# A graph transformer layer: the weighted sums take two slots per matmul, edge chunks go from five slots to six, and the prologue's matmuls are issued ahead of their evictions

## The chip, the cores and the metric

The kernel runs on one core of a Trainium2 chip. The metric is the time on the device, in microseconds (us), of one execution of the whole program; before the change it is the median of three runs.

The engines are called PE (TensorE, matrix products), Vector or DVE, ACT (ScalarE), POOL (GpSimd) and SP (SyncE, which here only issues DMAs). Transfers that are issued by POOL and gather or scatter rows by an index are called indirect DMAs. PSUM is the accumulator memory that PE writes[...].

## What is computed

One layer of a graph transformer over 6250 nodes with 256 features in float32. The 206,250 edges are sorted by destination and contain a self loop for each node, so a node has about 33 incoming edges.

```python
xn = layernorm(x)
# graph attention over the edges, 8 heads of 32
q, k, v = (xn @ W.T + b for W, b in ((Wq, bq), (Wk, bk), (Wv, bv)))
sim  = einsum('hed,hed->eh', q[:, dst], k[:, src]) * scale
p    = exp(sim - segment_max(sim, dst)[dst])
attn = p / segment_sum(p, dst)[dst]
agg  = segment_sum(attn * v[src], dst) @ Wo.T + bo
# linear attention over all nodes, 8 heads of 64, keys and values with instance norm
mix  = (qm @ (km.T @ vm) / 6250) @ w_out.T + b_out
x    = x + agg + mix
# top-1 mixture of 8 experts, 256 -> 1024 -> 256, each with a capacity of 1.25 * 6250 / 8
x    = x + experts(layernorm(x))
```

## The kernel before, in words

**Layout of the edges.** A block is 128 nodes, one in each partition; there are 49 blocks (`NB`). The nodes are ranked by their number of edges, so that the nodes of one block have about equally many. The ranking is done in three groups of 20, 17 and 12 blocks (`GROUPS`, L31). A block has as many slots as its longest node has edges; slot j of a block holds the j-th edge of each of its 128 nodes. The blocks have 1715 slots together, most of them 24 to 43, and three 62. A slot is one indirect DMA on POOL (L602): 128 rows of 512 float32, key and value, taken from the table `kv_tab` in device memory by the source indices `idx`. A block of more than 44 slots (`PART`) is cut into two units; there are 52 units. A unit is cut evenly into chunks of at most `W` = 5 slots (L559), 366 chunks in all, and a chunk is a tile `kvg` of the pool `kvp`, which has `RING` = 11 buffers (L25, L26, L202).

**Prologue.** For each block b, PE forms keys and values, `bank<-wn,xT` (L519, two matmuls of 512 columns, each of which appears in the trace as two records), Vector evicts them with norm and bias, `kv<-bank,rstd,bn` (L530), and SP writes them to `kv_tab` (L533). The statistics of the layer norm are made on ACT from rows of x, `xg`; these and the transposed x, `xT`, come by `load_x` (L368), four blocks at a time, issued by ACT's queue. Between the blocks `index_step` (L501) takes a piece of the ranking of the first group: `rank_group` (L266), with Vector's `lo`, `hi` and `rhs` (L332, L337, L344) and the matmuls that take them (L348). All of PE's products here take banks of the pool `bps` (five banks, function `bank`, L208), in the order in which the program gives them. Then POOL gathers the chunks of the first unit, while PE, Vector and SP do the same for the queries (L616, L620, L623) into `q_tab`. Both kinds of rows lie in three buffers (`ap3`) on their way out. Last, POOL gathers the queries of the first two blocks, and the loop begins.

**The loop over units.** It runs as if the unit before and the present one were interleaved. In one iteration, with c as the number of the chunk in each unit:

1. `weigh(v, c)` for the unit before: Vector multiplies the chunk's values by the weights `pr` (L1283), and PE adds the slots up by an identity matrix, 256 columns a slot, into `pa` in PSUM (L1287). The chunk's buffer is free after that.
2. `gather_to(at + 1 + LEAD)`: POOL issues the gathers of the chunk that lies `LEAD` = 2 chunks ahead, which needs a free buffer of the ring.
3. Scores of the present unit: Vector multiplies the keys by the queries (L1329) and reduces by head (L1330) into `sim`.

Around these steps `background` takes pieces of other work from a list: the ranking of the other groups, the linear attention, and, when a group of blocks has been sent, its output projection, routing, experts and last sum (`behind`, L1230). How much it takes at a time follows from `pace`, a hand-made estimate. After a unit's chunks come its maximum, the exponentials `pr` (L1347) and then `complete(v)` for the unit before: Vector multiplies `pa` by the inverse sums `s` into `ag` (L1303), and POOL scatters `ag` to the table `agg_tab` (`send`, `spaced_scatter`, L801). Each engine takes its instructions in the order in which the program issues them, POOL with its gathers and scatters too. So a scatter that waits for `ag` holds up the gathers behind it, and a unit with n chunks keeps n buffers of the ring until its weighing, one iteration after another, gives them back.

**The end.** The experts of the last group come after all gathers; their weights are loaded through the buffers of the same ring, `AHEAD` = 7 phases before their use (L1093). The kernel also has a general path for inputs that do not fit the plan; it does not run here.

Of the kernel before, what the change touches and what calls it, by code (L numbers as in the profile page):

```python
# [18 lines left out]
P = 128  # L19
# [5 lines left out]
W = 5  # L25
RING = 11  # L26
# [42 lines left out]
def gps_layer(  # L69
# [82 lines left out]
    with tc.manual_schedule():  # L152
# [52 lines left out]
        qps = mctx.enter_context(tc.tile_pool(name="qps", bufs=1, space=PSUM))  # L205
# [153 lines left out]
        with ExitStack() as actx:  # L359
            ap1 = actx.enter_context(tc.tile_pool(name="a1", bufs=1))  # L360
            ap2 = actx.enter_context(tc.tile_pool(name="a2", bufs=2))
            ap3 = actx.enter_context(tc.tile_pool(name="a3", bufs=3))

# [4 lines left out]
            def load_x(k, rows_too=True, queue=nc.scalar):  # L368
# [5 lines left out]
                if rows_too:  # L374
                    xg = ap2.tile([P, GX, D], F32, name="xg")
                    xgs[k] = xg
                    full = n
                    if b0 + n == NB:
                        full = n - 1
                        nc.vector.memset(xg[:, full, :], 0.0)  # L380
                        queue.dma_start(xg[:tail, full, :], x[(NB - 1) * P : N, :])
                    if full:
                        queue.dma_start(
                            xg[:, :full, :], x[b0 * P : (b0 + full) * P, :].rearrange("(t p) d -> p t d", p=P)
                        )
# [10 lines left out]
            load_x(0, queue=nc.sync)  # L396
            bn = ap1.tile([P, 3 * D], F32, name="bn")
            nc.sync.dma_start(bn, bcast_row(b_node, 3 * D))
            load_x(1, queue=nc.sync)
            for c in range(DC):  # L400
                nc.sync.dma_start(wn[:, c, 2 * D :], w_node[c * P : (c + 1) * P, 2 * D : 3 * D])
            load_x(2, queue=nc.sync)
# [110 lines left out]

            stat_end(0)
            for b in range(NB):
                k = b // GX
                pkv = bank((2 * D,))
                for c in range(DC):
                    nc.tensor.matmul(  # L519
                        pkv, xTs[k][:, b % GX, c, :], wn[:, c, : 2 * D], start=(c == 0), stop=(c == DC - 1)  # L520
                    )
                if b % GX == 0 and k + 1 < NGX:
                    stat_square(k + 1)
                if b % GX == GX - 1 and k + 1 < NGX:
                    stat_end(k + 1)
                    load_x(k + 3)
                    if k + 2 < NGX:
                        stat_sum(k + 2)
                kv = ap3.tile([P, 2 * D], F32, name="kv")
                nc.vector.scalar_tensor_tensor(  # L530
                    kv, pkv, rstd[:, b : b + 1], bn[:, : 2 * D], op0=ALU.mult, op1=ALU.add
                )
                nc.sync.dma_start(kv_tab[b * P : (b + 1) * P, :], kv)  # L533
# [18 lines left out]
            for b in order:  # L552
# [3 lines left out]
                for i in range(n_p):  # L556
                    n = cut[i + 1] - cut[i]
                    n_ch = -(-n // W)
                    cuts = [cut[i] + n * k // n_ch for k in range(n_ch + 1)]  # L559
# [52 lines left out]
            for b in range(NB):  # L612
                k = b // GX
                pq = bank((D,))
                for c in range(DC):
                    nc.tensor.matmul(  # L616
                        pq, xTs[k][:, b % GX, c, :], wn[:, c, 2 * D :], start=(c == 0), stop=(c == DC - 1)
                    )
                q = ap3.tile([P, 2 * D], F32, name="kv")[:, :D]
                nc.vector.scalar_tensor_tensor(  # L620
                    q, pq, rstd[:, b : b + 1], bn[:, 2 * D :], op0=ALU.mult, op1=ALU.add
                )
                nc.sync.dma_start(q_tab[b * P : (b + 1) * P, :], q)  # L623
                if b % GX == GX - 1:
                    load_x(k + 3, False)
# [8 lines left out]

        bctx = ExitStack()
# [444 lines left out]
        def experts(gi):  # L1080
# [12 lines left out]
            AHEAD = 7 if last else 2  # L1093
# [180 lines left out]
        def weigh(v, c):  # L1274
# [4 lines left out]
            if c == 0:  # L1279
                v["pa"] = qps.tile([P, D], F32, name="pa")  # L1280
# [5 lines left out]
            for j in range(m):  # L1286
                nc.tensor.matmul(v["pa"], ident, kv[:, j, D:], start=(j0 + j == s0), stop=(j0 + j == s1 - 1))  # L1287

        def complete(v):

            if v["part"] + 1 < v["parts"]:
                nc.vector.tensor_copy(v["acc"], v["pa"])
                return
            ag = cp3.tile([P, D], F32, name="ag")
            pa = v["pa"]
            if v["part"]:
# [4 lines left out]
                nc.vector.tensor_add(old, old, pa)  # L1301
                pa = old
            nc.vector.tensor_tensor(  # L1303
                heads(ag), heads(pa), v["s"][:, :, None].to_broadcast([P, GH, GD]), ALU.mult
# [613 lines left out]
```

## Time and profile before

The profiler took one execution; it is a good deal longer than the runs without it.

| what | value |
|---|---|
| time, median of three runs | 3119.5 us (3118.4 to 3120.74) |
| the profiled execution | 3534.2 us |
| its span, first to last instruction | 3532.3 us |
| mean granted TensorE clock in it | 0.812 |
| DMA | 730.28 MB, mean 207 GB/s |
| of it the gathers and scatters by POOL (software queue) | 477.83 MB, 44.4% of 16 engines |
| keys and values in the prologue | 13 to 156 us |
| queries in the prologue | 157 to 248 us |
| first scores | at 253 us |
| last gather | at 3206 us |
| experts of the last group | from 3341 us |

By stage, with the busy time of each engine, its number of instructions, the granted clock of PE, the share of the 16 DMA engines and the GB/s moved:

| stage, us | PE | Vector | ACT | POOL | clock | DMA | GB/s |
|---|---|---|---|---|---|---|---|
| 0 to 157 | 118.82 | 75.89 | 60.59 | 49.60 (58) | 0.85 | 0.59 | 188 |
| 157 to 250 | 53.93 | 26.75 | 0.00 | 36.43 (39) | 0.79 | 0.74 | 241 |
| 250 to 1000 | 461.18 | 550.03 | 155.02 | 456.90 (491) | 0.79 | 0.60 | 183 |
| 1000 to 2000 | 649.61 | 633.12 | 158.53 | 626.39 (692) | 0.81 | 0.67 | 207 |
| 2000 to 3000 | 694.10 | 573.52 | 140.02 | 600.46 (661) | 0.82 | 0.69 | 224 |
| 3000 to 3240 | 171.64 | 125.14 | 33.07 | 125.79 (138) | 0.81 | 0.61 | 199 |
| 3240 to 3532 | 188.45 | 39.07 | 86.62 | 24.39 (36) | 0.84 | 0.60 | 214 |

How to read the page: a group of instructions is named by its line, its engine and the tiles that it writes and reads, `pa<-kvg,ident`; then come the number of instructions, their busy time, the mean of one in ns, and the idle time of the engine just before them with what ended most of it. "issue" is idle time that ended with nothing the profile shows. The busy time of POOL's indirect DMAs is the time to issue them, not that of the transfer.

### The profile page before, as it was taken

Reading aid. Unit: us, or ns where it says so; the run is one execution under the profiler, and the core shown is the slowest. Engines: PE = TensorE matmul, PEld = TensorE weight load, DVE = VectorE, ACT = ScalarE, POOL = GpSimd, SP = SyncE. Lnnn points to the kernel's source line nnn. Section 1 sums busy time; section 2 is a strip of 40 time slices with the busy share of each in tenths; the row PEclk is TensorE's granted clock in tenths of the full one; section 3 lists DMA queues with packets and bytes.
Section 4 is the critical chain, followed back from the end, with each engine's and each line's share of the span. In section 5 each row is a group of like instructions: output and inputs, shape, how many; then the busy total and the mean of one; then the engine's idle time right before and its main releaser. Section 6 shows DMA issues by size and latency. Waiting matters only on the chain.

```text
span 3532.3 us, 29535 instructions
## 1 busy us (share of the span) xinstructions
PE 2337.7 (66%) x9086; PEld 1777.0 (50%) x9086; DVE 2023.5 (57%) x2723; ACT 633.9 (18%) x1802; POOL 1920.0 (54%) x2114
## 2 busy tenths in 40 slices
PE   7844457775767643764688887743664988866395
PEld 3433335443444432553576676622543877755394
DVE  4438677776767756676565654555673655545200
ACT  4200013322323200220111111110210111111142
POOL 4243656665666656656665665566546665552101
PEclk8876678888888876896798898866876999887697
DMA  6563956655655655775777776565756887664584
GB/s 215 197 205 103 332 156 182 181 173 168 181 172 176 185 160 167 240 218 176 254 253 241 241 247 230 183 195 176 234 162 215 287 271 255 237 201 139 199 321 141
DMA packets 291643, 730.28 MB, mean 207 GB/s; under 512 B 46838, under 2 KB 152020, under 8 KB 278164
## 3 DMA queue, kind: packets, MB, share of 16 engines
q0 software_dynamic: 149744, 477.83, 44.4%
q1 hardware_dynamic: 133560, 234.37, 18.9%
q10 hardware_dynamic: 8172, 16.10, 1.5%
q8 instruction: 75, 1.23, 0.1%
q14 instruction: 92, 0.75, 0.1%
HBM read 654.47 MB, written 73.64 MB: 206 GB/s over the span
## 4 chain that ended last, share of the span: by engine, by line
PE 38%; issue 20%; DVE 15%; POOL 12%; another core or an unknown queue 6%; DMA 6%; ACT 2%; DVEq 0%; SPq 0%; POOLq 0%; ACTq 0%
PE pa L1287 13%; POOL kvg L602 10%; PE bank L1145 8%; PE bank L1162 8%; DVE kvg L1329 3%; DVE sim L1330 3%; DVE kvg L1283 3%; PE bank L709 2%; DMA kvg<-kv_tab,idx 2%; PE bank L519 2%; PE bank L866 1%; PE bank L1166 1%; PE bank L746 1%; DMA q_tab<-kv 1%
## 5 line engine op out<-in xcount | busy, mean ns | idle before, releaser
L602 POOL DMA_INDIRECT kvg<-kv_tab,idx x1715 | 1624.9, 947 | 900.7 <-issue 466.4
L1287 PE MATMUL pa<-kvg,ident 128*128 128x256 f32 x3430 | 1026.8, 454 | 646.8 <-issue 413.7
L1287 PEld LDWEIGHTS pa<-kvg,ident 128*128 128x128 f32 x3430 | 765.3, 229 | 893.2 <-issue 493.9
L1329 DVE TENSOR_TENSOR kvg<-kvg,qc 128x1280 f32<-128x1280 f32 (+1 forms) x366 | 512.3, 1400 | 334.6 <-DMA kvg<-kv_tab,idx 248.0
L1330 DVE TENSOR_REDUCE sim<-kvg 128x40 f32<-128x1280 f32 (+1 forms) x366 | 513.2, 1402 | 12.6
L1283 DVE TENSOR_TENSOR kvg<-kvg,pr 128x1280 f32<-128x1280 f32 (+1 forms) x366 | 509.5, 1393 | 0.0
L1162 PE MATMUL bank<-wt,hTe 128*128 128x256 f32 x1056 | 269.2, 396 | 44.4 <-issue 43.6
L1145 PE MATMUL bank<-xTe,wt 128*128 128x256 f32 x1056 | 271.0, 405 | 33.8 <-issue 30.3
L1145 PEld LDWEIGHTS bank<-xTe,wt 128*128 128x128 f32 x1056 | 214.3, 204 | 79.1 <-issue 45.6
L1162 PEld LDWEIGHTS bank<-wt,hTe 128*128 128x128 f32 x1056 | 207.2, 199 | 85.0 <-issue 57.2
L1303 DVE TENSOR_TENSOR ag<-pa,s 128x256 f32<-128x256 f32 x46 | 19.5, 423 | 349.8 <-PE pa L1287 242.8
L709 PE MATMUL bank<-wm,xTm 128*128 128x512 f32 x392 | 193.2, 637 | 2.5 <-issue 2.4
L801 POOL DMA_INDIRECT agg_tab<-ag,node_ri x49 | 48.5, 989 | 248.1 <-DVE ag L1303 214.2
L1226 DVE TENSOR_TENSOR res<-bank,row_b 128x256 f32<-128x256 f32 x49 | 20.6, 421 | 270.4 <-ACT bank L1222 222.3
L1151 ACT ACTIVATE hTe<-bank,wt 128x256 f32<-128x256 f32 x264 | 108.0, 474 | 374.6 <-PE bank L1145 134.5
L1205 POOL DMA_INDIRECT row_a<-ybuf,row_from x49 | 46.6, 951 | 199.3 <-issue 190.7
L746 PE MATMUL bank<-ck,cv 128*128 128x128 f32 x392 | 75.6, 340 | 97.7 <-ACT ck L738 82.0
L718 ACT ACTIVATE sq<-bank 128x512 f32<-128x512 f32 x98 | 57.0, 595 | 420.5 <-PE pa L1287 157.5
L746 PEld LDWEIGHTS bank<-ck,cv 128*128 128x128 f32 x392 | 68.2, 241 | 113.4 <-ACT ck L738 90.1
L1168 ACT COPY res<-bank 128x256 f32<-128x256 f32 x85 | 31.6, 372 | 503.1 <-issue 230.5
L709 PEld LDWEIGHTS bank<-wm,xTm 128*128 128x128 f32 x392 | 78.9, 212 | 83.8 <-issue 83.5
L726 DVE TENSOR_REDUCE rv<-sq 128x16 f32<-128x1024 f32 x49 | 59.5, 1214 | 103.2 <-ACT sq L718 71.2
(254 smaller groups left out, 2258.7 us busy)
## 6 DMA issues: line engine op xcount, KB each, us to landing
wt<-in_w_rows_dram SPq DMA_DIRECT2D x33, 1152.0 KB
wt<-in_w_rows_dram SPq DMA_DIRECT2D x33, 1028.0 KB
kvg<-kv_tab,idx POOLq DMA_INDIRECT x1715
kvg<-in_w_rows_dram SPq DMA_DIRECT2D x19, 1152.0 KB
kvg<-in_w_rows_dram SPq DMA_DIRECT2D x19, 1028.0 KB
kv_tab<-kv SPq DMA_DIRECT2D x49, 256.0 KB
in<-xbuf SPq DMA_DIRECT2D x85, 128.0 KB
ybuf<-res SPq DMA_DIRECT2D x85, 128.0 KB
```

What stands on the lines that cost most here:

```text
L519: nc.tensor.matmul(pkv, xTs[k][:, b % GX, c, :], wn[:, c, : 2 * D], start=(c == 0), stop=(c == DC - 1))
L602: nc.gpsimd.indirect_dma_start(out=kv[:, j - j0, :], out_offset=None, in_=kv_tab[:, :], in_offset=bass.IndirectOffsetOnAxis(ap=idx_of[b][: ...
L709: nc.tensor.matmul(pm, xT_of[b][:, c, :], wmf[:, c, s * MI : (s + 1) * MI], start=(c == 0), stop=(c == DC - 1),)
L726: nc.vector.tensor_reduce(rv, sqs[b], AX.X, ALU.add)
L746: nc.tensor.matmul(dots[:, hp, :], cvs[b][:, h], ckf[:, h], start=(b == 0 and hp == 0), stop=(b == NB - 1 and hp == HP - 1), skip_group_ch ...
L1145: nc.tensor.matmul(ph[:, k, :], w[:, c, f * P : (f + 1) * P], T[t]["xT"][:, c, :size], start=(k == 0 and c == 0), stop=(k == 1 and c == DC ...
L1151: nc.scalar.activation(T[t]["hT"][:, f, :size], ph[:, k, :], AF.Relu, bias=w1_t[:, V1 + f : V1 + f + 1])
L1162: nc.tensor.matmul(py, T[t]["hT"][:, f, k * P : (k + 1) * P], w[:, f, :], start=(f == 0), stop=False)
L1283: nc.vector.tensor_tensor(vals, vals, v["pr"][:, j0 - s0 : j1 - s0, :, None].to_broadcast([P, m, GH, GD]), ALU.mult)
L1287: nc.tensor.matmul(v["pa"], ident, kv[:, j, D:], start=(j0 + j == s0), stop=(j0 + j == s1 - 1))
L1329: nc.vector.tensor_tensor(keys, keys, qc[:, None, :].to_broadcast([P, j1 - j0, D]), ALU.mult)
L1330: nc.vector.tensor_reduce(sim[:, j0 - s0 : j1 - s0, :], keys.rearrange("p j (h d) -> p j h d", d=GD), AX.X, ALU.add)
```

## The change

It has four parts.

1. **The sums of the values.** `pa` becomes a whole PSUM bank, two rows of 256 columns. One matmul takes two slots, 512 columns, so even slots of a pair add up in the first half and odd ones in the second; the last slot of a chunk with an odd number goes alone into the first half. `complete` adds the halves by a reduce that reads PSUM.
2. **Chunks of six.** `W` is 6 and `RING` 9, 54 slots of buffer after 55. The cuts between the chunks of a unit are rounded to even numbers of slots. There are 311 chunks after 366, and 841 paired and 33 single matmuls after 1715.
3. **The prologue's matmuls.** The keys of block b + 2 are multiplied after the eviction of block b, in three PSUM banks of their own (`aps`), and the queries of block b + 3 likewise. The pool `qps` is opened after the prologue to make room for these banks. Rows on their way to the tables have six buffers (`ap6`). All `load_x` go to SP's queue and come later in the order, and the rows of x lie in buffers of the ring.
4. **The last experts' weights** are loaded 6 phases ahead, as the ring has nine buffers.

```diff
@@ -22,8 +22,8 @@
 FLT_MAX = 3.4028234663852886e38
 GH, GD = 8, 32
 MH, MD = 8, 64
-W = 5
-RING = 11
+W = 6
+RING = 9
 LEAD = 2
 PART = 44
 GROUPS = (20, 17, 12)
@@ -202,7 +202,6 @@
         kvp = mctx.enter_context(tc.tile_pool(name="kvp", bufs=RING))
         cp3 = mctx.enter_context(tc.tile_pool(name="c3", bufs=3))
         cp2 = mctx.enter_context(tc.tile_pool(name="c2", bufs=2))
-        qps = mctx.enter_context(tc.tile_pool(name="qps", bufs=1, space=PSUM))
         bps = mctx.enter_context(tc.tile_pool(name="bps", bufs=5, space=PSUM))
 
         def bank(shape):
@@ -360,19 +359,22 @@
             ap1 = actx.enter_context(tc.tile_pool(name="a1", bufs=1))
             ap2 = actx.enter_context(tc.tile_pool(name="a2", bufs=2))
             ap3 = actx.enter_context(tc.tile_pool(name="a3", bufs=3))
+            ap6 = actx.enter_context(tc.tile_pool(name="a6", bufs=6))
+            aps = actx.enter_context(tc.tile_pool(name="aps", bufs=3, space=PSUM))
 
             GX = 4
             NGX = -(-NB // GX)
             xgs, xTs = {}, {}
 
-            def load_x(k, rows_too=True, queue=nc.scalar):
+            def load_x(k, rows_too=True, queue=nc.sync):
 
                 if k >= NGX:
                     return
                 b0 = k * GX
                 n = min(GX, NB - b0)
                 if rows_too:
-                    xg = ap2.tile([P, GX, D], F32, name="xg")
+                    xg = kvp.tile([P, W, 2 * D], F32, name="kvg")[:, :GX, :D]
                     xgs[k] = xg
                     full = n
                     if b0 + n == NB:
@@ -393,13 +395,13 @@
             wn = ap1.tile([P, DC, 3 * D], F32, name="wn")
             for c in range(DC):
                 nc.sync.dma_start(wn[:, c, : 2 * D], w_node[c * P : (c + 1) * P, : 2 * D])
-            load_x(0, queue=nc.sync)
+            load_x(0)
             bn = ap1.tile([P, 3 * D], F32, name="bn")
             nc.sync.dma_start(bn, bcast_row(b_node, 3 * D))
-            load_x(1, queue=nc.sync)
+            load_x(1)
             for c in range(DC):
                 nc.sync.dma_start(wn[:, c, 2 * D :], w_node[c * P : (c + 1) * P, 2 * D : 3 * D])
-            load_x(2, queue=nc.sync)
+            load_x(2)
             rc = rank_consts(ap1)
             sums = ap1.tile([P, 2, NB], F32, name="sums")
 
@@ -511,26 +513,37 @@
                 if b >= 8 + 5 * (need0 - 1) + 1:
                     next(ranks, None)
 
+            pkvs = {}
+            def keys_values(b):
+                if b >= NB:
+                    return
+                pkvs[b] = aps.tile([P, 2 * D], F32, name="pkv")
+                for c in range(DC):
+                    nc.tensor.matmul(
+                        pkvs[b], xTs[b // GX][:, b % GX, c, :], wn[:, c, : 2 * D], start=(c == 0), stop=(c == DC - 1)
+                    )
             stat_end(0)
+            keys_values(0)
+            keys_values(1)
             for b in range(NB):
                 k = b // GX
-                pkv = bank((2 * D,))
-                for c in range(DC):
-                    nc.tensor.matmul(
-                        pkv, xTs[k][:, b % GX, c, :], wn[:, c, : 2 * D], start=(c == 0), stop=(c == DC - 1)
-                    )
                 if b % GX == 0 and k + 1 < NGX:
                     stat_square(k + 1)
                 if b % GX == GX - 1 and k + 1 < NGX:
                     stat_end(k + 1)
+                kv = ap6.tile([P, 2 * D], F32, name="kv")
+                nc.vector.scalar_tensor_tensor(
+                    kv, pkvs.pop(b), rstd[:, b : b + 1], bn[:, : 2 * D], op0=ALU.mult, op1=ALU.add
+                )
+                nc.sync.dma_start(kv_tab[b * P : (b + 1) * P, :], kv)
+                if b % GX == GX - 1 and k + 1 < NGX:
                     load_x(k + 3)
                     if k + 2 < NGX:
                         stat_sum(k + 2)
-                kv = ap3.tile([P, 2 * D], F32, name="kv")
-                nc.vector.scalar_tensor_tensor(
-                    kv, pkv, rstd[:, b : b + 1], bn[:, : 2 * D], op0=ALU.mult, op1=ALU.add
-                )
-                nc.sync.dma_start(kv_tab[b * P : (b + 1) * P, :], kv)
+                keys_values(b + 2)
                 index_step(b)
             load_x(0, False)
             load_x(1, False)
@@ -556,7 +569,8 @@
                 for i in range(n_p):
                     n = cut[i + 1] - cut[i]
                     n_ch = -(-n // W)
-                    cuts = [cut[i] + n * k // n_ch for k in range(n_ch + 1)]
+                    cuts = [cut[i] + 2 * round(n * k / n_ch / 2) for k in range(n_ch)] + [cut[i + 1]]
                     units.append((b, i, n_p, cut[i], cut[i + 1], list(zip(cuts, cuts[1:]))))
             chunk_list = [(u, k) for u in range(len(units)) for k in range(len(units[u][5]))]
             UMAX = max(u[4] - u[3] for u in units)
@@ -609,20 +623,28 @@
             sources(1)
             gather_to(len(units[0][5]))
             less_mean(wn[:, :, 2 * D :], D)
-            for b in range(NB):
-                k = b // GX
-                pq = bank((D,))
+            pqs = {}
+            def query_rows(b):
+                if b >= NB:
+                    return
+                pqs[b] = aps.tile([P, 2 * D], F32, name="pkv")[:, :D]
                 for c in range(DC):
                     nc.tensor.matmul(
-                        pq, xTs[k][:, b % GX, c, :], wn[:, c, 2 * D :], start=(c == 0), stop=(c == DC - 1)
-                    )
-                q = ap3.tile([P, 2 * D], F32, name="kv")[:, :D]
+                        pqs[b], xTs[b // GX][:, b % GX, c, :], wn[:, c, 2 * D :], start=(c == 0), stop=(c == DC - 1)
+                    )
+            for b in range(3):
+                query_rows(b)
+            for b in range(NB):
+                q = ap6.tile([P, 2 * D], F32, name="kv")[:, :D]
                 nc.vector.scalar_tensor_tensor(
-                    q, pq, rstd[:, b : b + 1], bn[:, 2 * D :], op0=ALU.mult, op1=ALU.add
+                    q, pqs.pop(b), rstd[:, b : b + 1], bn[:, 2 * D :], op0=ALU.mult, op1=ALU.add
                 )
                 nc.sync.dma_start(q_tab[b * P : (b + 1) * P, :], q)
-                if b % GX == GX - 1:
-                    load_x(k + 3, False)
+                query_rows(b + 3)
+                if b % GX == 0 and b:
+                    load_x(b // GX + 2, False)
             queries(0)
             queries(1)
 
@@ -632,6 +654,7 @@
             nc.vector.tensor_reduce(bad[:, 0:1], down, AX.X, ALU.max)
 
 
+        qps = mctx.enter_context(tc.tile_pool(name="qps", bufs=1, space=PSUM))
         bctx = ExitStack()
         mp1 = bctx.enter_context(tc.tile_pool(name="m1", bufs=1))
         mp2 = bctx.enter_context(tc.tile_pool(name="m2", bufs=2))
@@ -1090,7 +1113,7 @@
             for t in range(1, n_t):
                 phases += [(0, t), (1, t - 1)]
             phases.append((1, n_t - 1))
-            AHEAD = 7 if last else 2
+            AHEAD = 6 if last else 2
 
             def load_w(i):
                 if i >= len(phases):
@@ -1277,31 +1300,39 @@
             m = j1 - j0
             kv = kv_of.pop((v["u"], c))
             if c == 0:
-                v["pa"] = qps.tile([P, D], F32, name="pa")
+                v["pa"] = qps.tile([P, 2, D], F32, name="pa")
             s0, s1 = v["s0"], v["s1"]
             vals = kv[:, :m, D:].rearrange("p j (h d) -> p j h d", d=GD)
             nc.vector.tensor_tensor(
                 vals, vals, v["pr"][:, j0 - s0 : j1 - s0, :, None].to_broadcast([P, m, GH, GD]), ALU.mult
             )
-            for j in range(m):
-                nc.tensor.matmul(v["pa"], ident, kv[:, j, D:], start=(j0 + j == s0), stop=(j0 + j == s1 - 1))
+            assert m > 1
+            for j in range(0, m - 1, 2):
+                nc.tensor.matmul(
+                    v["pa"], ident, kv[:, j : j + 2, D:], start=(j0 + j == s0), stop=(j0 + j + 2 == s1),
+                    skip_group_check=True,
+                )
+            if m % 2:
+                nc.tensor.matmul(
+                    v["pa"][:, 0, :], ident, kv[:, m - 1, D:], start=False, stop=(j1 == s1), skip_group_check=True
+                )
 
         def complete(v):
 
+            pa = v["pa"].rearrange("p t d -> p d t")
             if v["part"] + 1 < v["parts"]:
-                nc.vector.tensor_copy(v["acc"], v["pa"])
+                nc.vector.tensor_reduce(v["acc"], pa, AX.X, ALU.add)
                 return
             ag = cp3.tile([P, D], F32, name="ag")
-            pa = v["pa"]
+            nc.vector.tensor_reduce(ag, pa, AX.X, ALU.add)
             if v["part"]:
                 old = v["old"]
                 nc.vector.tensor_tensor(
                     heads(old), heads(old), v["corr"][:, :, None].to_broadcast([P, GH, GD]), ALU.mult
                 )
-                nc.vector.tensor_add(old, old, pa)
-                pa = old
+                nc.vector.tensor_add(ag, ag, old)
             nc.vector.tensor_tensor(
-                heads(ag), heads(pa), v["s"][:, :, None].to_broadcast([P, GH, GD]), ALU.mult
+                heads(ag), heads(ag), v["s"][:, :, None].to_broadcast([P, GH, GD]), ALU.mult
             )
             send(v["b"], ag)
 
```

## The prediction

> **What bounds the kernel now.** I read the first parts of the page, the groups by form, the waits, the stages of 250 us and the timeline of the first 250 us, in that order.
>
> ```profile
> PE 2337.7 (66%) x9086; PEld 1777.0 (50%) x9086; DVE 2023.5 (57%) x2723; ACT 633.9 (18%) x1802; POOL 1920.0 (54%) x2114
> ...
> L602 POOL DMA_INDIRECT kvg<-kv_tab,idx x1715 | 1624.9, 947 | 900.7 <-issue 466.4
> L1287 PE MATMUL pa<-kvg,ident 128*128 128x256 f32 x3430 | 1026.8, 454 | 646.8 <-issue 413.7
> ...
> L1303 DVE TENSOR_TENSOR ag<-pa,s 128x256 f32<-128x256 f32 x46 | 19.5, 423 | 349.8 <-PE pa L1287 242.8
> ```
>
> No engine is full by its share. But a gather takes 0.947 us and 0.30 us pass before the next, 1.25 us a slot; so the stages have to be read with that period:
>
> ```profile
> 500.00:750.00 250.00, 176.29 (x582) 116.63 (x580) 177.72 (x214) 72.22 (x215) 163.98 (x177) 0.86 0.62 182
> ...
> 1750.00:2000.00 250.00, 203.63 (x820) 166.40 (x818) 136.66 (x129) 38.27 (x96) 152.05 (x165) 0.87 0.74 242
> ```
>
> Each row: length, busy time (instructions) of PE, PEld, DVE, ACT, POOL, then PE clock, DMA share, GB/s. POOL's 177 and 165 instructions at 1.25 us are 221 and 206 us of 250: 82 to 88%. From 250 us to the last gather at 3206 us POOL issues 1678 gathers and about 216 other indirect DMAs: 1894 x 1.25 = 2368 us of 2956. The profiled execution (3534.2 us) is 414.7 us longer than the median of the runs, 3119.5; if most of that lies in this loop, POOL is over 90% full there in an ordinary run. So I hold the loop to be bound by POOL's gathers, and what counts in it is what holds POOL up:
>
> ```profile
> POOL agg_tab L801 <- DVE ag L1303: 214.2, 33, 15.0
> ...
> POOL kvg L602 <- PE pa L1287: 163.9, 55, 10.1
> ```
>
> (Sum, times, longest.) The first is POOL's in-order queue behind the scatter of a block's sums, the second a gather that waits for a buffer. Ahead of the loop lies the prologue, where a serial chain is to be seen:
>
> ```profile
> 95.06 0.73 DVE L530 SCALAR_TENSOR_TENSOR kv<-bank,rstd,bn 128x512 f32<-128x512 f32 x1
> ...
> 98.94 3.25 PE L348 MATMUL bank<-rhs,lo 128*128 128x60 f32 x14 [4.58 <-DVE rhs L344]
> ...
> 101.97 3.14 PE L519 MATMUL bank<-wn,xT 128*128 128x512 f32 x4
> ...
> 105.15 0.75 DVE L530 SCALAR_TENSOR_TENSOR kv<-bank,rstd,bn 128x512 f32<-128x512 f32 x1 [6.19 <-PE bank L519]
> ...
> 115.45 0.75 DVE L530 SCALAR_TENSOR_TENSOR kv<-bank,rstd,bn 128x512 f32<-128x512 f32 x1 [6.21 <-issue]
> ...
> 124.40 0.75 DVE L530 SCALAR_TENSOR_TENSOR kv<-bank,rstd,bn 128x512 f32<-128x512 f32 x1 [6.44 <-PE bank L519]
> ```
>
> Vector prepares a rank step, PE does it, only then does PE multiply the next block's keys, and Vector waits 6 us for them.
>
> **What the Trainium skill says.** "TensorE: Matmul & The Clock Gate", Back-to-back issue gap, puts the gap between matmuls at the columns over the clock and 2.5 ns. The trace agrees as to the proportion: 16 records of 256 columns take 3.46 us (216 ns each), and in the key stage the weight loads of 512-column records start 0.43 us apart. The same page, Part 1, lets PE fall to half rate after some 3.4 us of idleness; in the trace the granted clock is 0.50 from 270 to 310 us. "Perfetto Trace Analysis", Optimizing Scalar/DVE Operations, gives a Vector instruction a fixed cost; two forms of L1330 measure it here: 1486 ns for 1280 columns, 1220 for 1024, so 1.04 ns a column and 156 ns fixed. "Trainium Kernel Development and Optimization", Key Constraints: DMAs of all queues run on the same 16 engines, another queue saves only issue time. The trace has 0.35 to 0.5 us for an issue.
>
> **The change part by part.**
>
> *Wide matmuls.* 1715 slots were 1715 matmuls (two records each): 3430 x 216 ns = 741 us at full clock. Now 841 pairs and 33 single slots: 1682 x 432 + 66 x 216 ns = 741 us. PE streams the same columns; the gain is nothing at full clock. The L1287 mean of 454 is above 216 since it holds half clock and PE's waits for "issue". Whether those waits come with the number of instructions no row tells: bound 0 to -60 us (a seventh of the 414 us of "issue"); I take 0, as the experts' stage from 3341 to 3478 us runs at full pace without one.
>
> *Chunks of six.* By the planner's list 366 chunks become 311. Three Vector operations each: 55 x 3 x 156 ns = -26 us of Vector. *Halves added:* a reduce of 512 columns out of PSUM; nearest row L530, 512 columns from PSUM, 746 ns. 49 units x 0.75 + 3 first parts x 0.35 = +38 us. Vector nets +12 us, beside POOL, which covers it; uncovered at a block's end only.
>
> *A block's end.* POOL has LEAD = 2 chunks to issue before it meets the scatter: on average 2 x 4.7 slots, now 2 x 5.5: 2.1 us more cover. Vector's path to `ag` grows by a larger last chunk (0.5) and the reduce (0.75). Net 0.8 us better, for some of 33 waits: 0 to -26 us, I take -10.
>
> *The ring.* 11 x 5 slots become 9 x 6, nearly the same bytes, but a chunk is freed only when the previous unit's weighing has passed it, so what POOL may gather ahead is the ring less the previous unit's chunks. Units of 35 slots: 4 x 5 = 20 slots ahead, now 3 x 5.8 = 17.5. Of 37 to 39: 3 chunks (14), now 2 (11). Of 43: 2 (9.6), now 1 (5.4). The loop through the ring: a gather lands (3.6 us, as the chain of waits has it), scores 2 x 1.75, weighing 1.75, PE 6 x 0.43, then six gathers 7.5: 18.9 us. With one chunk ahead this covers two chunks, 9.5 us each against POOL's 7.5: 2 us x 8 chunks x 2 units = +32 us. With two ahead it is 6.3 us a chunk: it fits, but with 3.6 us to spare for all background work over three chunks; ten units are in this state. Before, four units had 16.5 us for three chunks against 17.8. I take +20 net; bounds 0 (POOL's time is made up later) and +60.
>
> *Prologue, keys.* The matmuls run two blocks ahead in three banks of their own. The three rank steps of 10 us (95.06 to 124.40 = 29.3) become the rank chain alone: L332 1.08, L337 0.30, L344 0.73, L348 3.25 = 5.4 each: -13. The steps before them are Vector's own 2.8 us a block already: -3. Six buffers in place of three for rows on their way to the table: Vector waited 9.9 us for `kv_tab`, but DMA ran at 256 to 308 GB/s there: -4. The last 18 blocks are PE's 1.73 us each: unchanged. *x loads* go from ACT's queue to SP's, between the table writes: 24 issues of under 0.5 us, on a queue that is otherwise idle between blocks; a write waits at most 1 us behind two loads, and six buffers hide it. ACT loses its waits, which nothing but the statistics of groups two ahead needed.
>
> *Prologue, queries.* Vector waited 23.5 us for `q_tab`; six buffers and three blocks ahead save -6, since 160 to 190 us is DMA at 92 to 100%. The first transposed tiles are now behind the last key write on SP: +3. The prologue thus gives -23, bounds -8 and -40, all of it on the path, for POOL idles from 207 to 248 us until the queries are there.
>
> *Tail.* Expert weights 6 phases ahead, not 7: a pair of phases takes 7.65 us of PE (3341 to 3478 us, evenly), the DMA keeps up; 0, bound +5.
>
> Sum: 0 - 10 + 20 - 23 = -13 of the profiled time. Steps that are work hold in an ordinary run; the ring's and the scatter's waits I take there at half, as Vector and PE have fewer stalls of their own: -5 + 10 - 23 = -18, and 3119.5 - 18 = 3101 us is my forecast.
>
> **The rivals.** *A. The ring decides (slower).* Place: units of 37 to 43 slots, twelve of 52, and the stages with output and routing, 2500 to 2690 us, where POOL's waits come thickest. Price +32 and 7 us for each of ten units less 24 for what the four tight units cost before, then 20 in the busy stages: +98 at worst, +50 likely: 3119.5 + 50 - 23 = 3146 us. It decides once the ring costs more than 23 us. For it: POOL is nearly full and cannot make up. Against: in most units the free slots hardly change. *B. PE's instruction count matters:* "issue" and cold starts shrink with 1682 records fewer in the loop: -60 for them, -23 for the prologue, +20 for the ring: 3056 us. For: 413.7 us of such waits. Against: the even tail. *C. It does nothing in sum:* ring and prologue cancel but for 3 us, 3117; that is also the case if the query stage stays DMA-bound and the rank steps were covered.
>
> **How the numbers follow.** My forecast 0.45, A 0.28, B 0.14, C 0.13. About 0.2%, 6 us, can be told from no change. Faster: B and the forecast less 0.02 at its edge, 0.57. Same: 0.15, which is C and that edge. Slower: A, 0.28. The range reaches from near B's value, 3065, to just above A's, 3150; outside lie about half of B and 0.12 of A, 0.19 together. The likeliest case alone is 3085 to 3113, and since A has the other sign, that is the range to hold it to.
>
> **What would show it.** Right: the first scores at some 225 us instead of 253; 512-column records at 430 ns or more; the reduce at about 0.75 us; POOL's waits on `pa` not above 200 us. Wrong: gathers in the units of 43 and 37 to 41 slots paced at 9 us a chunk, or a loop shorter by over 50 us at the same number of gathers.

## The result, and the profile after

| kernel | median | lowest to highest | ratio to before, 95% interval |
|---|---|---|---|
| before | 3120.12 us | 3118.4 to 3122.37 (4 runs) | |
| after the change | 3174.47 us | 3167.91 to 3178.84 (4 runs) | 1.0172 (1.0153 to 1.0191) |

The change makes the kernel 54 us slower. The forecast was 3101 us, its range ended at 3150.

The profile of before that the prediction read, and the runs e1 to e5 below, were taken while the kernel before took 3530 to 3550 us in place of 3120; this does not belong to the chip, as some expectations below have it, for one chip gave it 3533 us at one time and 3121 us later. The profile after is therefore set against a profile of before that was taken anew, beside it on one chip (f4 and f1 below).

The page of the kernel before, taken anew (span 3122.7 us): busy time, then the costliest groups.

```profile
PE 2236.5 (72%) x9086; PEld 1739.2 (56%) x9086; DVE 2026.6 (65%) x2723; ACT 640.2 (21%) x1802; POOL 1920.6 (62%) x2114
...
L602 POOL DMA_INDIRECT kvg<-kv_tab,idx x1715 | 1626.1, 948 | 675.6 <-issue 425.1
L1287 PE MATMUL pa<-kvg,ident 128*128 128x256 f32 x3430 | 1015.6, 453 | 580.9 <-DVE kvg L1283 444.1
```

The same of the changed kernel (f1, span 3180.8 us).

```profile
PE 2219.1 (70%) x7404; PEld 1352.0 (43%) x7404; DVE 2043.2 (64%) x2607; ACT 640.8 (20%) x1802; POOL 1928.8 (61%) x2114
...
L616 POOL DMA_INDIRECT kvg<-kv_tab,idx x1715 | 1631.8, 951 | 799.1 <-issue 446.9
L1311 PE MATMUL pa<-kvg,ident 128*128 128x512 f32 x1682 | 1004.9, 743 | 630.1 <-DVE kvg L1306 416.3
```

The sums have half the records, and PE's time in them stays nearly the same: 1015.6 us before, 1004.9 after and 22.6 more for the single slots (L1316, shown further below). What moves most is POOL's idle time ahead of its gathers, 675.6 us before, 799.1 after. Two stages of 250 us in which nothing else gets in the way, first of before, then of after (columns as in the prediction):

```profile
500.00:750.00 250.00, 202.97 (x729) 137.17 (x728) 219.38 (x265) 92.30 (x277) 189.74 (x205) 0.92 0.71 211
1750.00:2000.00 250.00, 207.97 (x906) 175.68 (x904) 170.69 (x167) 41.62 (x107) 186.96 (x202) 0.93 0.82 271
```

```profile
500.00:750.00 250.00, 194.50 (x530) 91.27 (x529) 217.38 (x245) 88.16 (x268) 189.90 (x205) 0.92 0.71 210
1750.00:2000.00 250.00, 229.31 (x839) 159.32 (x838) 179.71 (x154) 42.35 (x104) 190.00 (x206) 0.96 0.85 287
```

POOL issues 202 to 206 instructions in 250 us in both kernels, with 1.25 us from start to start: full. In most of the loop the change does nothing. The difference lies in the waits of POOL, before and after (sum in us, times, longest):

```profile
POOL kvg L602 <- PE pa L1287: 92.0, 94, 9.4
POOL agg_tab L801 <- DVE ag L1303: 54.7, 12, 15.2
```

```profile
POOL kvg L616 <- PE pa L1311: 156.9, 51, 20.4
...
POOL agg_tab L824 <- DVE ag L1334: 25.3, 6, 15.7
```

Gathers wait longer for the sums that free a buffer, scatters less for `ag`. The view names a releaser for each wait, and a wait for a buffer can stand under several names. Adding up all of POOL's gaps beyond the usual 0.30 us, from the first scores to the last gather, by what came after the gap, gives the following balance. The scatters are those of the sums, `agg_tab`, and those of the routing, `xbuf`; "loop" is the time between the first two columns.

| kernel | first scores | last gather | loop | gaps before gathers | gaps before scatters | rest of the gaps | time of the runs |
|---|---|---|---|---|---|---|---|
| before (f4) | 231 | 2793 | 2562 | 124 | 56 | 8 | 3119.5 |
| after (f1) | 194 | 2852 | 2658 | 252 | 20 | 10 | 3179.35 |
| f2, chunks of six alone | 234 | 2883 | 2649 | 247 | 16 | 10 | 3208.78 |
| f3, after with chunks of five | 191 | 2758 | 2567 | 122 | 63 | 6 | 3086.15 |
| i1, new prologue alone | 189 | 2749 | 2560 | 121 | 58 | 7 | 3083.2 |
| h1, after with units of 36 | 186 | 2787 | 2601 | 67 | 137 | 2 | 3121.95 |
| h2, f3 with units of 40 | 192 | 2753 | 2561 | 70 | 113 | 6 | 3088.84 |
| h3, h2 with ten buffers | 193 | 2793 | 2600 | 130 | 89 | 7 | 3115.04 |
| i2, f3 with a later scatter | 191 | 2757 | 2566 | 160 | 11 | 26 | 3102.11 |
| i3, h2 with a later scatter | 190 | 2749 | 2559 | 83 | 76 | 25 | 3081.64 |

In the kernel before, POOL issues 1892 indirect DMAs in the loop; at 1.25 us that is 2365 us, and with 189 us of gaps 2554 of the loop's 2562 us. After: 1889, 2361 us, with 281 us of gaps 2642 of 2658. The loop is POOL's own time and its gaps, and little else. The two executions differ by 58 us in span (the medians by 60 us in these runs, by 54 in the result above): 37 us are won ahead of the first scores and 96 lost in the loop, of which the gaps are 92. What follows the last gather is the same, 330 and 329 us.

Where the gaps grew: the table's 127 us more before gathers lie at few places. The gaps before the gathers of the block that follows the block of 43 slots in each of the first two groups went from 14 to 25 us and from 12 to 44 us; those of the other large blocks and halves at the head of the second and third groups from 0 to 7, 2 to 15, 1 to 10, 3 to 15 and 11 to 32; the start from 37 to 48. The chief one in POOL's timeline, before and after (idle time before the instruction and its releaser in brackets):

```profile
1341.71 1.00 POOL L801 DMA_INDIRECT agg_tab<-ag,node_ri  x1 [7.42 <-DMA x_tab<-row_b]
...
1347.40 0.97 POOL L602 DMA_INDIRECT kvg<-kv_tab,idx  x1 [4.58 <-PE pa L1287]
...
1357.28 0.94 POOL L602 DMA_INDIRECT kvg<-kv_tab,idx  x1 [3.91 <-PE pa L1287]
...
1364.53 0.94 POOL L602 DMA_INDIRECT kvg<-kv_tab,idx  x1 [1.31 <-PE pa L1287]
```

```profile
1335.02 0.94 POOL L616 DMA_INDIRECT kvg<-kv_tab,idx  x1 [0.31 <-issue]
1356.37 0.95 POOL L616 DMA_INDIRECT kvg<-kv_tab,idx  x1 [20.41 <-PE pa L1311]
...
1375.06 0.97 POOL L616 DMA_INDIRECT kvg<-kv_tab,idx  x1 [10.06 <-PE pa L1311]
```

Before, a part of the wait lies ahead of the scatter (7.42 us); after, POOL comes to the scatter 20 us later and finds it ready. The stretch of the first wait in the changed kernel as a window:

```profile
1330.00:1356.00 26.00, 14.12 (x62) 10.05 (x61) 24.62 (x45) 9.15 (x19) 4.74 (x5) 0.87 0.41 123
```

POOL has five instructions in 26 us; Vector is busy for 24.62 of them. It does the scores of the last three chunks of the eight of the 43-slot unit, three steps of the output stage of the group before, and the unit's end: maximum, exponentials' sums (L1366 to L1391) and `ag` (L1327 to L1334). The unit before had six chunks, all weighed by then, so nothing frees a buffer until Vector weighs the first chunk of the 43-slot unit (L1306, at 1351.14 in the timeline) and PE adds it up from 1352.92.

### The profile page after: what moved, and what is told of

Same layout as the page of the kernel before. It is cut to its first block, busy times and chain, and to the rows that moved or that the text cites. A ratio compares the mean times of both kernels' runs of the same rounds, so it can differ in the third digit from the quotient of the medians.

```text
span 3166.1 us, 26568 instructions
## 1 busy us (share of the span) xinstructions
PE 2205.7 (70%) x7404; PEld 1346.3 (43%) x7404; DVE 2042.8 (65%) x2607; ACT 638.6 (20%) x1802; POOL 1922.3 (61%) x2114
## 3 DMA queue, kind: packets, MB, share of 16 engines
q1 hardware_dynamic: 141732, 250.47, 22.6%
q8 instruction: 64, 1.05, 0.1%
## 5 line engine op out<-in xcount | busy, mean ns | idle before, releaser
L1311 PE MATMUL pa<-kvg,ident 128*128 128x512 f32 x1682 | 995.8, 737 | 627.3 <-DVE kvg L1306 422.9
L1311 PEld LDWEIGHTS pa<-kvg,ident 128*128 128x128 f32 x1682 | 371.1, 232 | 1132.8 <-DVE kvg L1306 552.4
L1360 DVE TENSOR_TENSOR kvg<-kvg,qc 128x1536 f32<-128x1536 f32 (+2 forms) x311 | 504.5, 1622 | 428.1 <-DMA kvg<-kv_tab,idx 354.4
L1361 DVE TENSOR_REDUCE sim<-kvg 128x48 f32<-128x1536 f32 (+2 forms) x311 | 504.9, 1624 | 10.7
L1306 DVE TENSOR_TENSOR kvg<-kvg,pr 128x1536 f32<-128x1536 f32 (+2 forms) x311 | 501.7, 1614 | 0.0
L1168 PE MATMUL bank<-xTe,wt 128*128 128x256 f32 x1056 | 241.3, 382 | 2.3 <-ACT xTe L1158 2.3
L824 POOL DMA_INDIRECT xbuf<-row_a,row_to x49 | 48.0, 980 | 93.2 <-DVE cmp L1069 66.9
L1154 PE MATMUL bank<-ident,in 128*128 128x128 f32 x170 | 28.6, 283 | 100.1 <-DMA in<-xbuf 100.1
L761 ACT ACTIVATE ck<-bank,rk 128x64 f32<-128x64 f32 x392 | 86.0, 341 | 37.4 <-DVE rk L758 37.4
L1282 ACT COPY qc<-qs 128x256 f32<-128x256 f32 x49 | 18.9, 386 | 368.0 <-DVE kvg L1360 266.7
L524 PE MATMUL pkv<-wn,xT 128*128 128x512 f32 x196 | 89.0, 606 | 4.6 <-DVE kv L538 4.6
```

The costliest lines, as they stand in the source:

```text
L524: nc.tensor.matmul(pkvs[b], xTs[b // GX][:, b % GX, c, :], wn[:, c, : 2 * D], start=(c == 0), stop=(c == DC - 1))
L761: nc.scalar.activation(cks[b][:, h, :], pms[b][0][:, h * MD : (h + 1) * MD], AF.Copy, scale=rk[:, h : h + 1])
L1168: nc.tensor.matmul(ph[:, k, :], w[:, c, f * P : (f + 1) * P], T[t]["xT"][:, c, :size], start=(k == 0 and c == 0), stop=(k == 1 and c == DC ...
L1306: nc.vector.tensor_tensor(vals, vals, v["pr"][:, j0 - s0 : j1 - s0, :, None].to_broadcast([P, m, GH, GD]), ALU.mult)
L1311: nc.tensor.matmul(v["pa"], ident, kv[:, j : j + 2, D:], start=(j0 + j == s0), stop=(j0 + j + 2 == s1), skip_group_check=True,)
L1360: nc.vector.tensor_tensor(keys, keys, qc[:, None, :].to_broadcast([P, j1 - j0, D]), ALU.mult)
```

## The experiments

Theory of the ring: a unit's chunks hold their buffers until they are weighed, chunks of six with nine buffers leave fewer for gathers ahead, and POOL, which bounds the loop, stands. Rivals: the wide matmuls with the added reduce; the new prologue; and, later, the coarser step of six slots itself.

**The parts by themselves (e1 to e4).** e1 is the kernel before, taken again. The others, changed lines alone:

```diff
 e2, on the kernel before
-W = 5
-RING = 11
+W = 6
+RING = 9
-                    cuts = [cut[i] + n * k // n_ch for k in range(n_ch + 1)]
+                    cuts = [cut[i] + 2 * round(n * k / n_ch / 2) for k in range(n_ch)] + [cut[i + 1]]
-            AHEAD = 7 if last else 2
+            AHEAD = 6 if last else 2
 e4, on the changed kernel: the same lines the other way round
 e3: e4 with weigh() and complete() as before, so that the new prologue alone is left
```

> The kernel before, unchanged, profiled once more. The first profile of it took 3534 us against runs of 3120 us; the profile after the change took 3168 us against 3174 us. If the first profile was a disturbed execution, this one takes about 3120 us, PE's 256-column records in the loop follow at 0.22 us without pauses of 0.7 us, POOL's gaps behind scatters fall from 232 us to under 100 us, and the gaps of gathers that wait for a buffer are under 249 us, which is what they are after the change. If the profiler itself costs this kernel 400 us, it takes 3500 us again.

> The kernel before with chunks of six, nine buffers and even cuts, one slot a matmul and the old prologue. Ring theory (a unit of 37 to 43 slots leaves one or two buffers for gathers ahead): the whole loss and what the prologue hides of it, 3180 to 3200 us. Theory of the wide matmuls (sums of 512 columns and the added reduce make each weighing and each block's end later): no loss here, 3110 to 3125 us. Theory of the prologue (rows of x in the ring, gathers held up at the start): 3115 to 3125 us.

> The kernel before with the new prologue alone (matmuls ahead, six buffers for rows, rows of x in the ring, all loads of x on SP); chunks of five, eleven buffers, one slot a matmul. Ring theory: 3090 to 3105 us, the gain that was forecast. Theory of the wide matmuls: the same, 3090 to 3105 us. Theory of the prologue: 3150 to 3175 us.

> The changed kernel with chunks of five, eleven buffers and the old cuts: the new prologue and the wide matmuls remain. Ring theory: the loss is gone and the prologue's gain is left, 3090 to 3110 us. Theory of the wide matmuls: 3155 to 3180 us, as after the change. Theory of the prologue: 3155 to 3175 us.

Measured: before 3551.74 us, e1 3551.24, e2 1.0038 (1.0022 to 1.0055), e3 0.994 (0.9917 to 0.9962), e4 0.9967 (0.9952 to 0.9982). e1 is neither of its two cases: it took as long as the runs beside it without the profiler. The signs of the others are those of the ring theory, the sizes are not those of the 54 us; e2, e3 and e4 lie far outside every range that was given for them in us.

**The changed kernel again (e5).**

> The changed kernel, unchanged, once more, beside the kernel before on the same chip. The runs so far came from two chips: on one the kernel before takes 3120 us and the change costs 54 us; on the other the kernel before takes 3552 us, chunks of six cost 12 us, the prologue brings 21 us or less, and the prologue with the wide matmuls 12 us. If the parts add up on the second chip, the changed kernel takes 3545 to 3558 us there, within 0.3% of the kernel before. If the loss of 54 us is the same on every chip, it takes 3600 to 3612 us. On the first chip it takes 3168 to 3180 us again.

Measured: 0.9909 (0.9876 to 0.9942) of 3533.3 us, faster than either case; e2 and e4, from another chip, do not add up to it. The loss of 54 us does not show here, and nothing is concluded on its cause from e1 to e5; what e1 and e2 show of the prediction's base comes below.

**All four on one chip (f1 to f4).** The changed kernel, e2, e4 and the kernel before.

> The changed kernel beside the next three, all on one chip. Chips have shown two kinds of behaviour: on one kind the kernel before takes about 3120 us, on the other 3530 to 3550 us, and there PE issues in bouts only one instruction each 0.70 us. On the first kind: 1.015 to 1.019 of the kernel before. On the second: 0.988 to 0.995, since 1682 records fewer go through those bouts.

> Chunks of six with nine buffers alone, with one slot a matmul and the old prologue. Ring theory, on a chip of the first kind: 1.020 to 1.027 of the kernel before, as the ring's loss is all there and the prologue's gain is not. Theory of the wide matmuls: 0.998 to 1.003 there. On a chip of the second kind both say 1.002 to 1.006, as measured there before.

> The changed kernel with chunks of five, eleven buffers and the old cuts. Ring theory, on a chip of the first kind: 0.990 to 0.997 of the kernel before, the prologue's gain. Theory of the wide matmuls: 1.010 to 1.019 there. On a chip of the second kind: 0.995 to 0.998, as measured there before.

> The kernel before, for a profile on the same chip. On a chip of the first kind: 3118 to 3125 us, no bouts of PE instructions 0.70 us apart, and gaps of POOL's gathers behind a busy buffer of 80 to 180 us in sum after the first scores, where the changed kernel has 249 us. If these gaps are 249 us or more there too, the ring is not what costs the 54 us.

Measured, with before at 3119.54 us: f1 1.0179 (1.0162 to 1.0197); f2, chunks of six alone, 1.0283 (1.0266 to 1.03); f3, everything but these chunks, 0.9883 (0.9864 to 0.9903); f4 3124.59 us in its one run, with the gaps of the table. Chunks of six with nine buffers cost 3208.78 - 3119.54 = 89 us on the kernel before and 3179.35 - 3086.15 = 93 us within the change. The theory of the wide matmuls wanted f3 above 1.01, that of the prologue too (its range under e4); both fall. The ring's interval was right for the gaps (124 of the 80 to 180 us), but f2 and f3 each went a little beyond their forecasts.

**Buffers or the coarser step (h1 to h3).** In h1 the chunks stay at six, but no unit has more than six of them; in h3 chunks stay at five, and one buffer goes.

```diff
 h1, on the changed kernel
-PART = 44
+PART = 36
 h2, on f3
-PART = 44
+PART = 40
 h3, on h2
-RING = 11
+RING = 10
-            AHEAD = 7 if last else 2
+            AHEAD = 6 if last else 2
```

> The changed kernel with blocks of 37 to 43 slots cut in two units as well, so that no unit has more than six chunks and three of the nine buffers are always left for gathers ahead; chunks stay at six slots. Ring theory (it is the number of buffers left by the unit before that costs): on a chip where the kernel before takes 3120 us, the gaps of gathers behind a busy buffer fall from 252 us to 110 to 160 us, and the time from 3179 to 3100 to 3140 us, twelve more ends of units included. Rival (it is the coarser step: each gather, weighing and score waits for six slots in place of five): no gain, 3175 to 3200 us. On a chip where the kernel before takes 3530 us or more: 0.985 to 1.000 of it by either theory.

> The new prologue and the wide matmuls with chunks of five and eleven buffers, and blocks of 41 and 43 slots cut in two, so that no unit has more than eight chunks. Ring theory: the gaps after the blocks of nine chunks (15, 12, 29 and 11 us) shrink, 3060 to 3085 us where chunks of five without the cut gave 3086 us. Rival: four more ends of units cost, 3086 to 3100 us. On a chip of the slower kind: 0.985 to 0.998 of the kernel before.

> The kernel above with ten buffers in place of eleven, the last group's weights six phases ahead. Chunks are as they were, only a buffer is gone. Ring theory: units of eight chunks leave two buffers, as the changed kernel's units of seven did, so 30 to 60 us more than the kernel above, with the gaps behind busy buffers 40 us or more above its own. Rival (coarser chunks): within 6 us of the kernel above. On a chip of the slower kind: 0 to 0.6% above the kernel above.

Measured, with before at 3119.18 us: h1 1.0014 (1.0006 to 1.0022), h2 0.9903 (0.9885 to 0.992), h3 0.9986 (0.9977 to 0.9994). h1 takes back 3179 - 3122 = 57 of the 93 us with chunks of six, its added ends of units paid for, and h3 loses 26 us with chunks of five by a single buffer: most of the loss goes with the free buffers. Two expectations were off. h1's gaps before gathers fell further than foreseen, to 67 us, but those before scatters rose from 20 to 137; h3 has 60 us more before gathers and 24 less before scatters, and 26 us was below the 30 to 60 foreseen. h2 was a miss and fell into its rival's range: its gaps before gathers went from 122 to 70 us, those before scatters took the place, and the time stayed. That h1 remains 36 us above f3 is not split up between its twelve added ends of units, the step of six and the cuts at even slots (chunks of 4 and 6 in turn), which no run takes alone.

**The prologue alone, and the scatter (i1 to i3).** i1 is e3 once more. In i2 and i3 the scatter of a block's sums is issued after the gathers of the next unit's second iteration:

```diff
 complete(), i2 on f3 and i3 on h2
-            send(v["b"], ag)
+            late_sends.append((v["b"], ag))
 the loop over chunks
                     gather_to(at + 1 + LEAD)
+                    if c == 1 and late_sends:
+                        send(*late_sends.pop(0))
 ... (what is left over is sent after the loop)
```

> The new prologue alone (chunks of five, eleven buffers, one slot a matmul), on a chip where the kernel before takes 3120 us. There the new prologue with the wide matmuls takes 3086 us. If the wide matmuls bring nothing in the loop, as the prediction had it, this one takes 3076 to 3088 us, 0.986 to 0.990 of the kernel before. If their fewer records are what brings the gain, it takes 3095 to 3120 us. On a chip of the slower kind: 0.992 to 0.996, as measured there.

> The new prologue and the wide matmuls with chunks of five and eleven buffers, and the scatter of a block's sums issued one unit's two chunks later, so that POOL does not stand before it while Vector is still at the sums. POOL's gaps before scatters are 161 us without this. If they are time of the loop, 3030 to 3065 us. If the ring takes over at once (gathers that come earlier wait for buffers), 3075 to 3090 us. On a chip of the slower kind: 0.96 to 0.99 of the kernel before.

> The same with blocks of 41 and 43 slots cut in two: gaps behind busy buffers were 70 us there and before scatters 210 us. If both kinds of gap are time of the loop: 3000 to 3055 us. If one takes over from the other: 3075 to 3092 us. On a chip of the slower kind: 0.96 to 0.99 of the kernel before.

The 161 and 210 us of gaps before scatters in these expectations include scatters of the routing after the last gather; within the loop they are 63 and 113 us. Measured, with before at 3121.03 us: i1 0.9878 (0.9861 to 0.9894), i2 0.994 (0.9923 to 0.9956), i3 0.9879 (0.9862 to 0.9895). i1 is at f3's ratio: the wide matmuls bring nothing and cost nothing that shows. In i2 the gaps before scatters fell from 63 to 11 us, those before gathers rose from 122 to 160 and the others from 6 to 26; the loop stayed at 2566 us, and what follows the last gather grew from 331 to 340 us, 9 of the 16 us between the medians of f3 and i2; the rest is not traced. i2 came out above the 3075 to 3090 us that a takeover was to give; i3 came out as a takeover was to give. A wait before a scatter was here only the other face of a wait for a buffer.

The new prologue alone (i1), without any other part of the change, beats both kernels at 3083 us; f3 and i3 are not told apart from it.

## Why the prediction was wrong

**What bounds the loop: right.** POOL's gathers do: 2365 of the loop's 2562 us, 92%, where the prediction said over 90%.

**The ring: the step that failed.** The term was "+20 net" of the profiled time, halved to "+10" for an ordinary run, with bounds of 0 and +60. The gaps before gathers grew by 127 us; less the 36 us by which the scatters' gaps fell, they agree with the 89 to 93 us that the chunks cost. The mechanism and the place were as stated: the units of 37 to 43 slots, and what follows them. Three things made the number small.

First, the price was set on two units alone. The loop through the ring, 18.9 us, was put together from the chunk's own work: landing, scores, weighing, sums, gathers. For the ten units with two chunks ahead the prediction said "it fits, but with 3.6 us to spare for all background work over three chunks", and set no price there. The gaps before gathers, sorted by the unit that went before, are these: after the two units of 43 slots (priced at +32) 25 us before and 69 after the change; after the ten units, 63 and 114 (the start of the loop, 37 and 48, among them); after all others, 36 and 69. In the window above, behind a unit of 43 slots, the scores, the unit's end and the output stage together keep Vector busy for 24.62 of 26 us. Behind the 41-slot unit of the third group, from 2297 to 2345 us, Vector is busy for 36.77 of 48 us only, so what holds up the chunks there stays open.

Secondly, it took the loop as steady, one buffer freed in each iteration. Where a unit has eight chunks after one of six, two iterations and the unit's end pass with nothing to weigh; the wait of 20.41 us is that stretch.

Thirdly, it took the term over from the profile by halving it, "as Vector and PE have fewer stalls of their own". The chunks of six alone were measured on both bases. On the base of the profile that was read (e1 and e2), POOL's gaps before gathers grew from 351 to 485 us, those before scatters fell from 234 to 110, and the time grew by 0.38%, 13 us (8 to 20). That is near the +20 - 10 of the forecast in profiled time, but by luck: two terms, each far too small, that nearly cancel. In the timed runs (f4 and f2) the gaps before gathers grew by as much, 124 to 247 us, but the scatters had only 56 us to give up and fell to 16; the time grew by 89 us. What shrinks in an ordinary run is not what the ring adds but the scatters' waits that hid it, so the halving went the wrong way. The two chief waits in the view, in e1, in e2 and in f2 (those of f4 stand above):

```profile
POOL agg_tab L801 <- DVE ag L1303: 230.1, 36, 14.3
POOL kvg L602 <- PE pa L1287: 145.0, 50, 9.9
```

```profile
POOL kvg L602 <- PE pa L1287: 255.3, 72, 28.7
POOL agg_tab L801 <- DVE ag L1303: 98.8, 21, 14.1
```

```profile
POOL kvg L602 <- PE pa L1287: 185.7, 84, 19.7
...
POOL agg_tab L801 <- DVE ag L1303: 29.1, 5, 14.3
```

All three are read from the traces; the shares of the first two in the loss are not told apart.

Rival A had this mechanism and its place, with +50 for the price; 93 was measured, close to its "+98 at worst", which did set a price on the ten units. It also held that POOL "cannot make up", which the gaps show: 92 us more of them, 96 us more of loop. The sign that was named for the ring misled: POOL's waits on `pa` stayed under 200 us (156.9), but the timed kernel before has only 92.0.

**A block's end.** The term was -10, for the longer cover of two chunks of six. The gaps before scatters did fall, by 36 us, but i2 and h2 show that this is no gain of its own: POOL, held up for buffers, comes later to the scatter. The term should not have stood beside that of the ring as if the two added up.

**The wide matmuls: right.** Nothing was forecast; i1 without them is at 0.9878, f3 with them at 0.9883. Rival B's -60 is thereby gone. The reduce was put at 0.75 us; in the groups by form of the changed kernel it takes 686 ns (the middle line is that of the single slots):

```profile
L1327 DVE TENSOR_REDUCE ag<-pa 128x256 f32<-128x512 f32 x49 | 33.6, 686 | 78.2 <-PE pa L1316 52.7 <-PE pa L1311 25.4
...
L1316 PE MATMUL pa<-kvg,ident 128*128 128x256 f32 x66 | 22.6, 428 | 0.0
...
L1334 DVE TENSOR_TENSOR ag<-ag,s 128x256 f32<-128x256 f32 x49 | 20.9, 426 | 1.7
```

49 of them are 33.6 us of Vector beside a full POOL, where the sum had 36.8.

**The prologue: right in kind, too small.** -23 was forecast, bounds -8 and -40. The first scores come 37 us earlier, and i1 alone is 3121.03 - 3083.2 = 38 us faster. The rank steps in the changed kernel's timeline:

```profile
78.45 0.74 DVE L538 SCALAR_TENSOR_TENSOR kv<-pkv,rstd,bn 128x512 f32<-128x512 f32 x1
78.51 3.24 PE L347 MATMUL bank<-rhs,lo 128*128 128x60 f32 x14 [3.53 <-DVE rhs L343]
...
83.78 0.75 DVE L538 SCALAR_TENSOR_TENSOR kv<-pkv,rstd,bn 128x512 f32<-128x512 f32 x1
84.49 1.67 PE L347 MATMUL bank<-rhs,lo 128*128 128x60 f32 x14
```

The eviction no longer waits for PE; this rank step takes 83.78 - 78.45 = 5.3 us, where 5.4 was worked out. The last key is evicted at 119.7 us against 147.8, 28 us where 20 were forecast; the queries take 65 us against 77, 11 where 3 were forecast. The second is the larger miss for its size: before (f4), the share of the DMA engines falls from 0.99 to 0.64 and 0.56 after 200 us; in the changed kernel it is 0.97 to 1.05 from 140 to 180 us, at 332 to 406 GB/s (a slice counts the transfers that start in it, so a share can pass 1). The prediction took the whole stage as bound by DMA from its fullest part.

**The tail: right.** 330 and 329 us after the last gather.

**Rival C** fell with the prologue: 38 us are not hidden.

## What to carry to other kernels

When a ring of buffers is cut anew, count not bytes but the buffers that are free at the worst place: after the unit with the most pieces, in the stretch in which nothing is freed, with all the background work that runs there. If the engine that fills the ring is full, a gap there is hardly made up again: here 92 us of gaps made 96 us of loop. Waits of one in-order queue at different places can be one wait seen twice: take one away and look whether the next one grows before counting it as a gain. For the same reason a wait does not simply shrink with the stalls around it; look for what covers it in the profile, and ask whether that cover is there in the timed runs.

## What was not expected of the hardware

The DMA engines moved 394 to 406 GB/s for 30 us of the query stage, with gathers and table traffic together, where the kernel before had 333 to 367 GB/s in its fullest 40 us. And halving the records of a float32 sum of the same columns left PE's busy time the same to about 1% (1015.6 us for 3430 records of 256 columns; 1004.9 for 1682 of 512 and 22.6 for 66 of 256), though the weights of these sums were loaded half as often: 9086 and 7404 loads over the whole kernel.
